# A fused expert-and-category kernel on one core: GpSimd's additions in runs tied to VectorE, a plan for them by slot, and the gate's sums in chosen slots

## The chip, the core and the metric

The kernel runs on one core of one Trainium2 chip. The metric is device time in microseconds of one execution; three executions of the kernel before took 2267.85, 2266.24 and 2268.05, median 2267.85. One more execution was profiled, and every duration below comes from it.

Names of engines: PE is TensorE (PEld its weight loads), DVE is VectorE, ACT is ScalarE, POOL is GpSimd, SP is SyncE, which issues nearly all DMAs. L871 is line 871 of the kernel before.

## What is computed

Two sequences of 2048 tokens with 512 features, all fp32. Cut to what matters:

```python
def dense(x, wi, wo):
    return relu(x @ wi) @ wo                    # 512 -> 2048 -> 512
s0 = dense(x, swi[0], swo[0])                   # two shared experts
s1 = dense(x, swi[1], swo[1])
eo = dense(x, wi[label[b]], wo[label[b]])       # one chosen expert for each sequence
gate_in = concatenate([eo[:, 0], s0[:, 0], s1[:, 0]])     # first token only
w = softmax(relu(gate_in @ g1) @ g2)            # 3 weights for each sequence
x = x + eo * w[0] + s0 * w[1] + s1 * w[2]
out = x + x @ W[cat[b]] + bias[cat[b]]          # a 512 x 512 layer for each sequence
```

## The kernel before

**Units.** Tokens are cut into 4 blocks of 1024. A unit is one expert on one block, 12 in all: units 0 to 3 are shared expert 0 on the four blocks, 4 to 7 shared expert 1, 8 and 9 the chosen expert of sequence 0, 10 and 11 that of sequence 1. Each unit has an up phase (`up`, 512 to 2048, relu) and a down phase (`down`, 2048 to 512).

**Fast multiplication.** Each product is done by two nested levels of a scheme with 7 block products in place of 8, paid for with sums and differences of blocks. So there are sums of the weights (`Prep`), sums of x (`x_sums`), sums of the hidden values (`make_tops` L701 to L708, `outer_sum` L871, the wide sums L744), and sums of results (L783 to L813 in the up phase, L914 to L933 in the down phase, `y_sums` L877). An up phase is 7 outer items in the order 1, 6, 2, 5, 7, 4, 3, each of 14 slots (`SEQ_UP`): 98 slots of 4 matmul instructions (L766), some 0.86 us each. A down phase is 49 slots (`SLOTS_DN`) of 8 matmul instructions (L900), some 1.73 us each, named by item and inner product: (7, y5) is slot 24, (4, x6) slot 43, (4, y5) slot 44. In an up phase items 1 and 5 "store" (ACT copies results out of PSUM), the others add results to an earlier block on DVE.

**The order of work is written by hand** (`tc.manual_schedule`). After each slot's matmuls and its evictions the program issues, in this order: wide sums, x sums (one step of `xg`), tops, the paced preparation (`prep_paced`), then one step of the background list `other_bg`. Each engine works its own list off in this order, and waits only for data and free buffers.

**Preparation of weights.** For shared expert 1 and both chosen experts (3 x 2 matrices of 4 groups each) `Prep` reads a group of raw weights by eight DMAs (L179, tile `pr`), makes 12 sums of it on GpSimd (L141: four `po`, four `ps`, four `pt`), and stores them to DRAM (L228) three slots after the last sum of each kind. 24 groups make 288 additions. `prep_paced` counts slots up by a rate (`RATE_UP` by item, `RATE_DN` by item) and issues one addition each time a whole one is reached; nothing but data and buffers holds the addition back on GpSimd. The first group of all is issued in unit 1, the last additions in unit 8. Of the 288, 59 are issued in down phases of units 1 to 7, and 29, 30, 29, 29, 29, 29, 29, 25 in the up phases of units 1 to 8.

**x sums.** Units 0 to 4 (`MAKES`) make the sums of their x block on GpSimd as they go (L370, L356), one item ahead of the matmuls that read them (`xi`, `xt`), and units 1 to 4 store them (`keep_parts`) for later units, which load them (`fetch_parts`).

**Weights of the matmuls** come by SP from DRAM into a pool of 12 tiles (`fetch_w`, L469 to L488); a load is issued when the tile twelve weights earlier has been used.

**Gate and layer 1.** When the chosen expert has done the first block of a sequence (units 8 and 10), `gate` and `layer1` of the block before are put in `other_bg`, one step of it a slot. The gate multiplies the rows of g1 by `gate_in` on DVE (twelve instructions, L1018 and L1020, one a slot from its ninth step on), sums over partitions by a matmul, multiplies by g2 (L1032, three), reduces all three at once (L1035), and makes the softmax (L1037 to L1047, with one Exp on ACT). `layer1` follows: 8 tiles, each with three scalings on ACT (L1112), three additions on GpSimd (L1117, `mix`), 4 matmuls (L1080, `po`) and one DVE addition with the bias (L1088). In unit 11, `premix` prepares the last block: it loads `acc` and four halves (`pm`), and adds them with 16 DVE instructions (L1158), one a step; what is left of `other_bg` at slot 47 of the last down phase is issued there. `last_mix` (L1170) adds the chosen expert's part tile by tile, and `last_layer1` ends the kernel with 64 `po` matmul instructions.

In unit 9 and unit 11 the gate's steps run from up item 1 slot 0 to item 3 of the order (item 2), slot 2; `layer1` from there to slot 4 of the down phase; in unit 11 `premix` from there to slot 32. In unit 10 there is `layer1` alone, up to the up phase's sixth item.

Of the kernel before, what the change touches and what calls it, by code (L numbers as in the profile page):

```python
# [8 lines left out]
F32 = mybir.dt.float32  # L9
AF = mybir.ActivationFunctionType  # L10
ALU = mybir.AluOpType
AX = mybir.AxisListType
# [3 lines left out]
P = 128  # L16
# [20 lines left out]
def cond_resid_kernel(  # L37
# [106 lines left out]
    class Prep:  # L144
# [89 lines left out]
        def step(self):  # L234

            self.flush(clock[0])
            done = bool(self.p) and (len(self.p) != 12 or clock[0] >= self.since + 6)
            if done:
                self.p.pop(0)()
            self.more()  # L240
            return done

        def more(self):
# [401 lines left out]

    pace = [0.0]

    def prep_paced(rate):
        clock[0] += 1
        if prep_bg:  # L650
            prep_bg[0].flush(clock[0])
        pace[0] = min(pace[0] + rate, 4.0) if prep_bg else 0.0
        while prep_bg and pace[0] >= 1 and prep_step():
            pace[0] -= 1

# [55 lines left out]
    def up(n, xg, tops, y):  # L711
# [12 lines left out]
        for j, i in enumerate(I_UP(n)):  # L724
# [32 lines left out]
            for s, (bk, k, d) in enumerate(SEQ_UP):  # L757
# [77 lines left out]
                if s in top_at:  # L835
                    next(tg, None)
                prep_paced(RATE_UP[j])
                step(other_bg)
# [10 lines left out]
    def down(n, H, tops, y, prepare):  # L849
# [124 lines left out]
        for s, (i, name) in enumerate(SLOTS_DN):  # L974
            if s in at:
                for _ in job:
                    pass
                job = jobs[at[s]]()
                y_sums(0, *sums.get(at[s], ()))
            elif s in second:  # L980
                y_sums(1, *sums.get(second[s], ()))
            slot(i, name)
            next(job, None)
            if name == "z2" and i != 1:
                next(job, None)
            prepare(s)
            prep_paced(RATE_DN[i])
            step(other_bg)
# [9 lines left out]
        nc.sync.dma_start(out=ys[slot_y, blk], in_=yf)  # L998

    gin = [const.tile([P, NX, DC], F32, name=f"gin_{b}") for b in range(B)]  # L1000
    gates = {}

    def gate(b, lag):
# [10 lines left out]
        for k in range(NX * DC):  # L1014
            j, c = divmod(k, DC)
            col = gin[b][:, j, c : c + 1]
            if k == 0:
                nc.vector.tensor_scalar(hid, g1t[j][:, c, :], col, None, ALU.mult)  # L1018
            else:
                nc.vector.scalar_tensor_tensor(hid, g1t[j][:, c, :], col, hid, ALU.mult, ADD)  # L1020
            yield
        for _ in range(3):
# [6 lines left out]
        yield  # L1029
        prod = bigp.tile([P, NX, D], F32, tag="o", bufs=1, name=f"prod_{b}")  # L1030
        for j in range(NX):
            nc.vector.tensor_tensor(prod[:, j, :], act, g2b[:, :, j], ALU.mult)  # L1032
            yield
        logit = small.tile([P, NX], F32, tag="logit", name=f"logit_{b}")
        nc.vector.tensor_reduce(logit, prod, AX.X, ALU.add)  # L1035
        mx = small.tile([P, 1], F32, tag="mx", name=f"mx_{b}")
# [98 lines left out]
    def premix(blk, lag):  # L1135
# [19 lines left out]
        for k, (j, h) in enumerate(parts):  # L1155
            for c in range(DC):
                o = acc["t"][c // 2][:, c % 2, h * 512 : (h + 1) * 512]
                nc.vector.scalar_tensor_tensor(  # L1158
                    o, got[k][:, c, :], gates[b][:, j : j + 1], o, ALU.mult, ADD
                )  # L1160
                yield
            if k == 0:
                fetch(3)
# [21 lines left out]

    RATE_UP = [0.36, 0.34, 0.34, 0.34, 0.18, 0.18, 0.34]
    RATE_DN = {1: 0.0, 2: 0.0, 3: 0.1, 7: 0.4, 6: 0.0, 5: 0.25, 4: 0.45}

    with tc.manual_schedule():
# [16 lines left out]
        for n, (e, blk) in enumerate(units):  # L1206
# [48 lines left out]
            if e >= 2:  # L1255
# [5 lines left out]
                if blk % NBB == 0:  # L1261
                    other_bg.append((f"g{b}", gate(b, 8)))
                if n + 1 < len(units):
# [34 lines left out]
```

## Time and profile before

| what | value |
|---|---|
| median of three runs | 2267.85 us |
| the profiled execution | 2268.57 us |
| its span, first to last instruction | 2266.8 us |
| mean granted TensorE clock | 0.995 |
| POOL L141 additions | 288, some 416 us in all |
| POOL x sums L370 | 140, 127 us |
| DVE adds with both operands in SBUF: L871, L744, L701 to L708 (t) | 192 x 1330, 96 x 1497, 288 x 1364 ns |
| DVE adds with one operand in PSUM: L789, L794, L813 | 240 x 686, 168 x 691, 168 x 687 ns |

A phase below is named by its stretch of the span in us. The page gives busy time and number of instructions of each engine; an answer by stretches gives the same for each stretch, with the granted clock, the DMA share and GB/s at the end of the line. An answer for one line of the kernel gives its instructions with their least, median and greatest duration in ns, and the first and last start. A list of waits says which engine stood still for which instruction, how long in total, how often, and the longest time. PE's busy time has modelled ends: single matmuls of 128x256 are shown with some 380 ns and start 216 ns apart, so the length of a phase says more than PE's busy time in it.

### The profile page before, as it was taken

What the parts mean: (1) busy time and instruction counts of PE and PEld (TensorE: products, weight loads), DVE (VectorE), ACT (ScalarE), POOL (GpSimd) and SP (SyncE); (2) the same over time, 40 slices, a digit from 0 to 9 for tenths busy, and PEclk for the clock granted to TensorE, in tenths of its full rate; (3) what the DMA queues carried; (4) which work ended last, traced back from release to release, by engine and by line L of the source; (5) the groups of instructions that cost most, each with busy time, mean ns of one, the idle gap of its engine ahead of it and who ended that gap; (6) DMA issues with size and microseconds to landing.
All of it is one profiled execution on the core that took longest, in us unless ns stands there. A gap on an engine that the chain in (4) does not pass through costs nothing.

```text
span 2266.8 us, 28546 instructions
## 1 busy us (share of the span) xinstructions
PE 2200.3 (97%) x9808; PEld 1852.5 (82%) x9808; DVE 1662.8 (73%) x2010; ACT 545.3 (24%) x937; POOL 790.5 (35%) x598
## 2 busy tenths in 40 slices
PE   8899999999999999999999999999999999999999
PEld 6787888888888888788888888888877877887686
DVE  7897787678588688588588588577676746857685
ACT  3221231331321320131231131131133133213310
POOL 6777543642752752332153233230032023002300
PEclk9999999999999999999999999999999999999999
DMA  9543997997996997796996896895896697579671
GB/s 339 194 172 98 354 316 231 305 324 233 339 327 191 309 309 218 262 321 191 292 324 184 281 330 189 291 326 161 285 310 187 185 306 239 154 239 326 211 274 56
DMA packets 483339, 577.22 MB, mean 255 GB/s; under 512 B 28280, under 2 KB 316024, under 8 KB 479740
## 3 DMA queue, kind: packets, MB, share of 16 engines
q1 hardware_dynamic: 478924, 567.53, 77.6%
q10 hardware_dynamic: 4272, 7.87, 1.0%
q8 instruction: 80, 1.31, 0.2%
q14 instruction: 63, 0.52, 0.1%
HBM read 417.47 MB, written 157.81 MB: 254 GB/s over the span
## 4 chain that ended last, share of the span: by engine, by line
PE 75%; DVE 11%; DMA 4%; issue 2%; POOL 1%; SPq 1%; ACT 0%; POOLq 0%; DVEq 0%; ACTq 0%
PE dx L900 21%; PE ux L766 19%; PE dy L900 11%; PE uy L766 9%; PE dz L900 5%; PE po L1080 5%; PE uz L766 5%; DVE h L871 2%; DVE y L877 1%; DVE t L701 1%; DVE t L706 1%; DVE t L704 1%; DMA w<-ws_s 1%; DMA g1raw<-in_L_cond_g_dram 1%; DVE hid L1020 1%
## 5 line engine op out<-in xcount | busy, mean ns | idle before, releaser
L900 PE MATMUL dx<-t,w 128*128 128x256 f32 x1680 | 399.4, 381 | 10.6 <-DVE ds L922 10.3
L766 PE MATMUL ux<-xs,w 128*128 128x256 f32 x1568 | 376.5, 381 | 10.4 <-DVE sm L1043 3.2
L900 PEld LDWEIGHTS dx<-t,w 128*128 128x128 f32 x1680 | 318.3, 190 | 58.8 <-DVE ds L922 12.4
L766 PEld LDWEIGHTS ux<-xs,w 128*128 128x128 f32 x1568 | 295.2, 190 | 66.3 <-DVE us L789 7.8
L1117 POOL TENSOR_TENSOR mix<-mix 128x512 f32<-128x512 f32 x72 | 101.4, 1409 | 536.9 <-ACT mix L1112 354.7
L141 POOL TENSOR_TENSOR po<-pr 128x384 f32<-128x384 f32 x48 | 59.3, 1250 | 601.1 <-DMA w<-ws_t 211.6
L871 DVE TENSOR_TENSOR h<-h,h 128x1024 f32<-128x1024 f32 x192 | 252.5, 1330 | 0.0
L789 DVE TENSOR_TENSOR us<-ux,h 128x512 f32<-128x512 f32 x240 | 162.3, 686 | 119.2 <-PE ux L766 118.9
L738 ACT ACTIVATE h<-h 128x1024 f32<-128x1024 f32 x156 | 164.5, 1056 | 239.3 <-DVE h L794 112.8
L766 PE MATMUL ux<-xi,w 128*128 128x256 f32 x808 | 192.2, 381 | 15.2 <-DVE us L789 6.2
L794 DVE TENSOR_TENSOR h<-uy,us 128x512 f32<-128x512 f32 x168 | 116.0, 691 | 120.8 <-ACT us L787 116.6
L766 PE MATMUL uy<-xs,w 128*128 128x256 f32 x784 | 187.7, 380 | 4.2 <-DVE h L813 2.4
L800 ACT ACTIVATE h<-uz 128x512 f32<-128x512 f32 x168 | 99.6, 593 | 380.7 <-PE uz L766 372.6
L766 PEld LDWEIGHTS ux<-xi,w 128*128 128x128 f32 x808 | 151.9, 190 | 41.7 <-issue 13.3
L900 PE MATMUL dy<-h,w 128*128 128x256 f32 x672 | 162.3, 385 | 11.9 <-DVE y L924 11.9
L766 PEld LDWEIGHTS uy<-xs,w 128*128 128x128 f32 x784 | 148.4, 190 | 30.6 <-DVE h L813 4.6
L900 PEld LDWEIGHTS dy<-h,w 128*128 128x128 f32 x672 | 128.3, 192 | 32.4 <-DVE y L924 9.8
L813 DVE TENSOR_TENSOR h<-uy,us 128x512 f32<-128x512 f32 x168 | 113.0, 687 | 52.0 <-PE uy L766 49.8
L744 DVE TENSOR_TENSOR h<-h,h 128x1024 f32<-128x1024 f32 x96 | 143.7, 1497 | 6.5 <-ACT h L800 5.1
L900 PE MATMUL dx<-h,w 128*128 128x256 f32 x616 | 146.3, 380 | 0.0
L900 PE MATMUL dz<-h,w 128*128 128x256 f32 x616 | 145.6, 379 | 0.1
L900 PE MATMUL dy<-t,w 128*128 128x256 f32 x576 | 136.1, 379 | 0.0
(153 smaller groups left out, 3365.5 us busy)
## 6 DMA issues: line engine op xcount, KB each, us to landing
w<-ws_t SPq DMA_DIRECT2D x352, 256.0 KB, 4.1
w<-ws_s SPq DMA_DIRECT2D x270, 256.0 KB, 4.2
w<-ws_o SPq DMA_DIRECT2D x264, 256.0 KB, 5.2
xs<-xs SPq DMA_DIRECT2D x49, 896.0 KB, 7.2
ws_s<-ps SPq DMA_DIRECT2D x24, 1024.0 KB, 7.7
ws_t<-pt SPq DMA_DIRECT2D x24, 1024.0 KB, 7.8
ys<-y SPq DMA_DIRECT2D x11, 2048.0 KB, 8.5
ws_o<-po SPq DMA_DIRECT2D x24, 768.0 KB, 7.4
```

The source lines that it names most:

```text
L141: eng.tensor_tensor(o, i0, i1, op)
L738: nc.scalar.activation(v, v, AF.Relu)
L744: nc.vector.tensor_tensor(o, blk_of(O[22], cc), blk_of(O[21], cc), ADD)
L766: nc.tensor.matmul(p[:, g, :], lhsT=wt[:, 2 * d + g, :], rhs=x_ops[n, i, k], start=first and g == 0, stop=True, skip_group_check=True,)
L789: nc.vector.tensor_tensor(t, p, half(src, 12 if k == 6 else 22, d), ADD)
L794: nc.vector.tensor_tensor(half(dst, 22, d), bank["y", d], t, ADD)
L800: nc.scalar.activation(half(dst, 11, d), p, AF.Relu if i in final else AF.Copy)
L813: nc.vector.tensor_tensor(half(dst, 12, d), p, sn["b", d], ADD)
L871: nc.vector.tensor_tensor(bl(o), bl(i0), bl(i1), SUB)
L900: nc.tensor.matmul(p, lhsT=wt[:, g, :], rhs=op[g], start=first and g == 0, stop=True, skip_group_check=True,)
L1080: nc.tensor.matmul(po[t], lhsT=mixed[c], rhs=l1[blk][0][:, c, :], start=(c == 0), stop=(c == DC - 1),)
L1117: nc.gpsimd.tensor_tensor(m[:, 3, :, :], m[:, 3, :, :], m[:, j, :, :], ADD)
```

## The change

Three things change.

1. **Additions in runs, each tied to DVE.** `prep_paced` is split. `prep_tick` counts the slot and issues stores that are due. `prep_run(count)` issues up to `count` additions (and one more where some are owed, five owed at most). Ahead of the first one it has DVE write a one-element memset to `pulse`, and GpSimd read it by a one-element addition into `seen`, so that the run's additions come, on GpSimd, behind the DVE work issued before the memset. Also the begin of a next group of raw weights comes with a run, no longer with any slot. In the built program there are 139 such pairs.
2. **A plan by slot.** `RUN_UP` and `RUN_DN` replace the rates: in an up phase runs of 2 or 3 after slots 4 and 8 of each item, in a down phase 2 after (7, y5), and 2 each after (4, x6) and (4, y5) where the next unit makes no x sums. Units that make x sums (0 to 4) have a plan of their own: none in the first item, then 3 and 2, 2 and 1, 2 and 1, 3 and 2, 3 and 2, 3 and 3. In the built program 31 additions stand in down phases (2, 2, 3, 6, 6, 6, 6 in units 1 to 7), and 27, 27, 26, 27, 38, 38, 38, 36 in the up phases of units 1 to 8.
3. **Gate and premix.** The gate's products, multiplications by g2 and reductions are issued only when `quiet` is set: in slots 1, 2, 11, 12, 13 of an up item, and in any slot of a down phase; two products a step. The reduction is split in three. The lag is 6 for 8. `premix` issues two sums a step. In the built program the gate's steps now end at slot 0 of the fifth item (7) of unit 9's and unit 11's up phase, `layer1` ends at slot 30 of the down phase, and `premix` runs from slot 30 to slot 47, with its sums from slot 42 on and six of the 16 at slot 47.

The order of instructions on PE and ACT is otherwise as before.

```diff
+        def can(self):
+            return bool(self.p) and (len(self.p) != 12 or clock[0] >= self.since + 6)
...
-    pace = [0.0]
-
-    def prep_paced(rate):
+    PULSES = 64
+    pulse = const.tile([1, PULSES], F32, name="pulse")
+    seen = const.tile([1, 1], F32, name="seen")
+    pulses, debt = [0], [0]
+
+    def prep_tick():
         clock[0] += 1
         if prep_bg:
             prep_bg[0].flush(clock[0])
-        pace[0] = min(pace[0] + rate, 4.0) if prep_bg else 0.0
-        while prep_bg and pace[0] >= 1 and prep_step():
-            pace[0] -= 1
+
+    def prep_run(count):
+
+        if not prep_bg:
+            return
+        debt[0] = min(debt[0] + count, 5)
+        most = count + 1
+        ready = False
+        while prep_bg and debt[0] and most:
+            if prep_bg[0].can() and not ready:
+                k = pulses[0] % PULSES
+                pulses[0] += 1
+                mark = pulse[:, k : k + 1]
+                nc.vector.memset(mark, 0.0)
+                nc.gpsimd.tensor_tensor(seen, mark, mark, ADD)
+                ready = True
+            if not prep_step():
+                break
+            debt[0] -= 1
+            most -= 1
...
-                prep_paced(RATE_UP[j])
+                prep_tick()
+                prep_run(RUN_UP[n in MAKES][j].get(s, 0))
+                quiet[0] = s in (1, 2, 11, 12, 13)
                 step(other_bg)
...
-            prep_paced(RATE_DN[i])
+            prep_tick()
+            prep_run(RUN_DN[n + 1 in MAKES].get((i, name), 0))
+            quiet[0] = True
             step(other_bg)
...
+            while not quiet[0]:
+                yield
             if k == 0:
                 nc.vector.tensor_scalar(hid, g1t[j][:, c, :], col, None, ALU.mult)
             else:
                 nc.vector.scalar_tensor_tensor(hid, g1t[j][:, c, :], col, hid, ALU.mult, ADD)
-            yield
+            if k % 2:
+                yield
...
         for j in range(NX):
+            while not quiet[0]:
+                yield
             nc.vector.tensor_tensor(prod[:, j, :], act, g2b[:, :, j], ALU.mult)
             yield
-        logit = small.tile([P, NX], F32, tag="logit", name=f"logit_{b}")
-        nc.vector.tensor_reduce(logit, prod, AX.X, ALU.add)
+            while not quiet[0]:
+                yield
+            nc.vector.tensor_reduce(logit[:, j : j + 1], prod[:, j : j + 1, :], AX.X, ALU.add)
+            yield
...
                     o, got[k][:, c, :], gates[b][:, j : j + 1], o, ALU.mult, ADD
                 )
-                yield
+                if c % 2:
+                    yield
...
-    RATE_UP = [0.36, 0.34, 0.34, 0.34, 0.18, 0.18, 0.34]
-    RATE_DN = {1: 0.0, 2: 0.0, 3: 0.1, 7: 0.4, 6: 0.0, 5: 0.25, 4: 0.45}
+
+    RUN_UP = {
+        False: [{4: 3, 8: 3}] * 3 + [{4: 3, 8: 2}] * 4,
+        True: [{}, {4: 3, 8: 2}, {4: 2, 8: 1}, {4: 2, 8: 1}] + [{4: 3, 8: 2}] * 2 + [{4: 3, 8: 3}],
+    }
+    RUN_DN = {
+        False: {(7, "y5"): 2, (4, "x6"): 2, (4, "y5"): 2},
+        True: {(7, "y5"): 2},
+    }
...
-                    other_bg.append((f"g{b}", gate(b, 8)))
+                    other_bg.append((f"g{b}", gate(b, 6)))
```

## The prediction

> **What bounds the kernel now.** I read the page first, then the costs of single operations, then the phases, then the waits of TensorE. A unit is one up phase (98 slots) and one down phase (49 slots); its bounds are the first `ux` and `dx` matmuls of the timeline.
>
> ```profile
> PE 2200.3 (97%) x9808; PEld 1852.5 (82%) x9808; DVE 1662.8 (73%) x2010; ACT 545.3 (24%) x937; POOL 790.5 (35%) x598
> ```
>
> TensorE is the bound, so only time in which it waits can be won. Phases (from:to, us, then busy us of PE, PEld, DVE, ACT, POOL):
>
> ```profile
> 832.20:926.00 93.80, 87.19 (x393) 75.78 (x393) 70.97 (x76) 9.95 (x25) 21.75 (x12) 0.96 0.68 207
> ...
> 1011.30:1097.10 85.80, 84.80 (x393) 74.35 (x392) 68.68 (x76) 9.99 (x25) 20.03 (x12) 1.00 0.69 209
> 1097.10:1183.90 86.80, 85.23 (x394) 74.28 (x394) 59.65 (x79) 29.44 (x42) 33.56 (x24) 1.00 1.01 326
> 1183.90:1271.40 87.50, 85.13 (x394) 74.30 (x393) 71.15 (x76) 10.00 (x25) 23.67 (x12) 1.00 0.67 204
> ...
> 1357.80:1446.70 88.90, 86.60 (x394) 75.57 (x393) 70.82 (x76) 10.04 (x25) 19.69 (x10) 0.98 0.68 210
> ...
> 1533.40:1618.00 84.60, 84.60 (x393) 74.47 (x392) 62.81 (x76) 10.02 (x25) 0.00 (x0) 1.00 0.59 175
> 1618.00:1736.30 118.30, 113.71 (x453) 84.71 (x452) 78.01 (x113) 44.81 (x68) 33.19 (x24) 1.00 0.88 294
> ...
> 1824.40:1939.60 115.20, 114.06 (x459) 86.56 (x458) 66.56 (x92) 44.82 (x66) 33.60 (x24) 1.00 0.85 271
> ```
>
> The down phase of unit 8 has no POOL work and takes 84.6 us; those of units 4 to 7 run the same 76 DVE instructions with 10 to 12 POOL additions and take 93.8, 85.8, 87.5 and 88.9. DVE is busy 8 us longer in them for the same work. Why, the instructions show (ns min/median/max):
>
> ```profile
> L871 DVE TENSOR_TENSOR h<-h,h x192: 1209/1218/2287, 127.9 to 2213.7; 128x1024 f32<-128x1024 f32 x192
> ...
> L789 DVE TENSOR_TENSOR us<-ux,h x240: 673/687/693, 40.8 to 2135.7; 128x512 f32<-128x512 f32 x120
> ...
> L141 POOL TENSOR_TENSOR ps<-pr x48: 1256/1277/2313, 217.9 to 1492.2; 128x512 f32<-128x512 f32 x48
> ```
>
> DVE's add of two SBUF tiles goes from 1.22 to 2.29 us, its add with a PSUM operand (`us<-ux`) never moves. The timeline of unit 4 shows both engines stretched together, and that POOL runs its 12 additions as one burst as soon as the raw weights land:
>
> ```profile
> 899.17 2.28 DVE L701 TENSOR_TENSOR t<-h 128x1024 f32<-128x1024 f32 x1
> 901.48 2.17 DVE L704 TENSOR_TENSOR t<-h,t 128x1024 f32<-128x1024 f32 x1
> ...
> 902.54 2.25 POOL L141 TENSOR_TENSOR ps<-ps,pr 128x512 f32<-128x512 f32 x1
> 904.86 2.12 POOL L141 TENSOR_TENSOR ps<-pr,ps 128x512 f32<-128x512 f32 x1
> ```
>
> There follows the longest wait of TensorE (us in total, times, longest), that for `y`:
>
> ```profile
> PE dy L900 <- DVE y L924: 11.9, 7, 6.3
> PE dx L900 <- DVE ds L922: 11.0, 11, 2.3
> ...
> PE ux L766 <- POOL xi L370: 1.2, 2, 0.9
> ```
>
> At the end, DVE is full exactly while premix (L1158) runs, and free after it:
>
> ```profile
> 2180.00:2195.00 15.00, 15.00 (x71) 13.20 (x70) 15.00 (x19) 2.29 (x6) 0.00 (x0) 1.00 0.78 275
> 2195.00:2210.00 15.00, 12.53 (x55) 9.77 (x54) 14.93 (x22) 1.14 (x3) 0.00 (x0) 1.00 0.42 122
> ...
> 2223.00:2235.50 12.50, 12.50 (x60) 11.00 (x59) 5.95 (x13) 0.77 (x2) 0.00 (x0) 1.00 0.00 0
> ```
>
> **What the Trainium skill says.** "SBUF — State Buffer", Who interferes with whom: a DVE instruction with two SBUF inputs contends with a GpSimd instruction that reads SBUF, one with at most one SBUF input doesn't, and the later one is blocked. The trace agrees (1.22 to 2.29 us against an unmoved 0.69). "TensorE: Matmul & The Clock Gate", Architectural detail: VectorE and GpSimd are strict FIFOs, so everything behind a waiting pulse waits too. "VectorE: DVE Perf Modes", The TRN2 errata: an fp32 tensor_tensor takes (N+151)/0.96 ns; 512 gives 691 (trace 687), one element 158.
>
> **Part 1, the pulses.** 139 memsets on DVE and 139 one-element adds on POOL, counted in the built program. No row shows them. DVE: the trace's reciprocal of one column took 0.16, like the 158 above; 139 x 0.16 = 22 us; DVE idles 25 to 30% of these phases and hides most of it. I take 2 us on the path (bounds 0 and 10; no gain is in a memset as such). POOL: from 128x256 at 0.73 and 128x512 at 1.28, one element is about 0.19: 26 us of an engine 35% busy, 0 on the path unless POOL fills up (rival 3). The new wait: POOL's one-element add stands until DVE has worked off what was issued before the memset. Behind it queue the run's additions, then x sums (L370, L356) of units 1 to 4, for which TensorE waits 2.5 slots into the next item; and SP waits for what those write.
>
> **Part 2, where the 288 additions go.** By the program 59 of them stood in down phases of units 1 to 7 and 31 do now: 2, 2, 3 in units 1 to 3, 6 in each of 4 to 7. Four of the six follow (4, x6) and (4, y5), where DVE has only PSUM adds and y_sums (L877) left; two at (7, y5) still meet the tops.
> - Down, units 4 to 7: 9.2 + 1.2 + 2.9 + 4.3 = 17.6 over 84.6. About a fifth of the meetings remain: 3.5. Gain 14 (bounds 9 and 17). Late next is DVE's own chain, which unit 8 hides wholly.
> - Down, units 1 to 3: 90.0, 89.0, 86.3. The first two hold 32 transposes of about 0.11 (3.5 us), so 1.9, 0.9, 1.7 are lost. x sums remain there: gain 2.
> - Up, units 1 to 4 (86.5, 89.6, 87.0, 87.4): 12.1 lost over 84.6. Item 1 of such units gets no additions and x sums come first, but they meet the wide sums as before: gain 2 (bounds -8 and 8). Units 5 to 8 (85.3, 86.8, 86.4, 86.7): 6.8 lost; they now take 38, 38, 38, 36 additions for 29, 29, 29, 25. A burst after slot 4 is over by slot 9; one after slot 8 (2 or 3 x 1.28, begun about 2 us late behind DVE's queue) lasts to slot 13 and meets wide sums at 11. I take 0 (bounds -4 and 5).
> - SP: a store of prepared weights is issued 3 slots (2.6 us) after its last addition, which can now end 6 us after its slot. SP stands about 3 us, with weight loads, x stores and raw loads behind it. Weights are 12 tiles, 20 us, ahead and land in 4 to 5: hidden. Without that cover each stop costs its 3 us.
> - Raw loads (L179, eight for each of 24 groups) are issued from a run too, not from any slot. Each lands in 3.4 us (median), and the group's first addition comes 6 to 14 slots later (5 to 12 us): 0 on the path; a late group shifts a run toward the wide sums (rival 2). Both orders end in unit 8, so nothing is forced at its end.
>
> **Part 3, the gate.** Unit 9's up takes 118.3 with 453 matmuls, unit 10's 115.2 with 459; six po matmuls are 6 x 0.43 = 2.6, so a gate costs 118.3 - 112.6 = 5.7, twice 11.4. The twelve products (0.75 each) now go in pairs to slots 1, 2, 11, 12, 13; six in slots 11 to 13 are 6 x 0.66 = 4.0 us of DVE beside 1.2 of its `h` sums, four more in slots 1 and 2 are 2.7 beside 1.2 of `uz`: 9.1 us of work in the 7.7 of nine slots, so DVE is about 1.5 behind at slot 4, and `sm` still waits for ACT's Exp. I leave 1.2 each: gain 9 (bounds 4 and 11). The shorter lag (6 for 8) costs 0: the first product now waits for slot 11 anyway, when the loads it used to wait 2.1 us for have landed. The split reduction adds 4 small instructions, within that.
>
> **Part 4, what the later gate pushes.** It ends 26 slots later (item 5 slot 0 instead of item 3 slot 2), and layer 1 with it: it ran to down slot 4 and now to slot 30. So 12 of 24 POOL mixes (four groups of three, 1.27 each) and 4 to 5 puts (0.69) fall among the tops and outer sums of the down phases of units 9 and 11. Units 5 to 7 lost 1.2 to 4.3 with 12 in longer bursts: 1.5 each, 3 in all (bounds 0 and 8). Unit 10 has no gate.
>
> **Part 5, the end.** premix starts 26 down slots later and its 16 sums stand in slots 42 to 47, six of them and four last_mix sums together at 47. DVE's pitch there is 0.66 and 0.42. From slot 42's eviction at 2225.1: 10.6 of sums, 1.7 of last_mix, 4.7 of its own work give the first finished tile near 2241, where TensorE wants it at 2235.5: +5.5. What premix cost at 2195 to 2210 (15.0 - 12.5 = 2.5) goes. Net +3 (bounds -2 and 9). Its loads keep their distance of ten slots and land in 8.2.
>
> **Sum.** -14 - 2 - 2 - 0 - 9 + 2 + 3 + 3 = -19. The profiled execution took 2268.57 (span 2266.8 and 1.8 around it), 0.7 above the median 2267.85. 2267.85 - 19 = 2249.
>
> **Rivals.**
> 1. Everything fits: the up phases recover 12 more and the tail 5: 2232. For it: unit 5's up lost only 0.7 with 24 additions. Against: the wide sums at slot 11.
> 2. The change doesn't separate the engines: a memset holds POOL back only until DVE gets there, and in items that store (1 and 5) DVE runs ahead, so bursts meet tops and wides after all; 12 of the 19 are given back: near 2261.
> 3. Slower: in items 5 and 6 of units 1 to 4 POOL has 5 additions, 4 x sums, 2 pulses: 5 x 1.28 + 4 x 0.73 + 0.4 = 9.7 of 12.1 us. If all are contended (2.28 and 1.72) it is 18.7, 6.6 late in each of two items, less 2.2 of lead: 11 a unit. At three quarters of that, 32 in four units: 2281. It decides from a mean addition of about 1.75 us. Against: `xi` waits are 1.2 us now.
>
> **Chances.** Forecast 0.61 (2238 to 2259), rival 1 0.14, rival 2 0.14, rival 3 0.11. A measurement tells 0.2% (4.5 us) from no change. Faster: 0.61 + 0.14 + 0.08 of rival 2; same 0.06; slower 0.11. The range 2230 to 2264 leaves out rival 3 and the edges.
>
> **What would show it.** Right: down phases of units 4 to 7 near 85.5, L871's and L701's means near 1.25, unit 9's up near 114 after its po matmuls are counted, a DVE full to the end of unit 11 and a gap before the last po matmuls. Wrong: TensorE waits for `xi` or for `w` above 5 us, or up phases of units 5 to 8 beyond 88.

## The result, and the profile after

The changed kernel takes 2287.34 us (median of 6 runs, 2282.66 to 2288.25) against 2267.95 for the kernel before: ratio 1.0075, 95% interval 1.0064 to 1.0086. By the medians it is slower by 19 us (14.5 to 19.5 by the interval) where 19 us less were forecast. Lines shift: L766 before is L789 after, L871 is L896, L744 is L767, L900 is L925.

The engines' busy times, from the page after:

```profile
PE 2199.9 (96%) x9808; PEld 1854.9 (81%) x9808; DVE 1676.0 (73%) x2153; ACT 545.1 (24%) x937; POOL 802.3 (35%) x737
```

TensorE's busy time over the whole span is what it was (2200.3 before), and the span is 18.4 us longer. The phases (from:to, length, busy us of PE, PEld, DVE, ACT, POOL with their instructions, clock, DMA share, GB/s): down of units 4 and 5, up and down of 6, down of 7 and 8, then up and down of 9:

```profile
837.00:922.20 85.20, 85.12 (x393) 74.33 (x393) 66.31 (x79) 10.03 (x25) 11.23 (x11) 1.00 0.76 239
1009.10:1099.80 90.70, 87.00 (x393) 75.40 (x392) 70.38 (x80) 9.98 (x25) 20.41 (x18) 0.98 0.74 227
1099.80:1187.70 87.90, 85.47 (x393) 74.15 (x392) 59.62 (x100) 29.38 (x42) 41.09 (x45) 1.00 1.02 332
1187.70:1284.60 96.90, 89.27 (x394) 76.69 (x393) 73.20 (x79) 10.00 (x25) 24.28 (x24) 0.95 0.68 208
1371.10:1459.50 88.40, 86.50 (x393) 75.53 (x392) 68.88 (x79) 10.01 (x25) 18.71 (x16) 0.98 0.71 219
1547.30:1631.90 84.60, 84.60 (x393) 74.47 (x393) 62.85 (x76) 10.03 (x25) 0.00 (x0) 1.00 0.66 200
1631.90:1734.50 102.60, 98.36 (x421) 79.13 (x421) 72.11 (x110) 37.62 (x56) 15.59 (x12) 1.00 0.89 296
1734.50:1838.30 103.80, 102.07 (x433) 82.02 (x433) 75.11 (x82) 17.35 (x37) 23.43 (x12) 1.00 0.61 187
```

Unit 4's down phase came out as forecast (93.8 to 85.2). Those of units 5, 6 and 7 hold 18, 24 and 16 GpSimd instructions where the plan has six additions and their pulses, and take 90.7, 96.9 and 88.4. The waits of TensorE tell what is new in them (us in total, times, longest; L925 are the down phases):

```profile
PE dz L925 <- DMA w<-in_L_cond_swo_dram: 8.4, 2, 5.9
PE dx L925 <- DMA w<-ws_o: 1.9, 2, 1.6
PE ux L789 <- DMA w<-ws_s: 1.4, 1, 1.4
PE uy L789 <- DMA w<-ws_o: 0.9, 1, 0.9
```

Weights are late, 13 us with the small ones, all but 0.3 of it in units 5 to 8. The longest wait cost more than its own length. After it the granted clock is at half for a while, and three us hold 9 matmuls in place of 15:

```profile
1214.00:1217.00 3.00, 3.00 (x9) 2.37 (x8) 0.00 (x0) 0.00 (x0) 0.00 (x0) 0.50 0.99 327
1220.00:1223.00 3.00, 3.00 (x15) 2.64 (x14) 2.10 (x4) 0.35 (x1) 0.00 (x0) 1.00 0.74 252
```

So unit 6's down phase takes 12.3 us more than unit 8's 84.6: 7.5 of waits, and 4.7 by which PE is busy longer (89.27) at a mean clock of 0.95. Units 5 to 8 together take 709.7 for 692.0: TensorE's waits for weights grew from 2.0 to 12.7 there, those for VectorE stayed at some 8, and PE's busy time grew from 682.0 to 688.4. Why the weights are late, SyncE's timeline across unit 6 shows (start, us the issue takes):

```profile
1178.47 4.50 SPq L179 DMA_DIRECT2D pr<-in_L_cond_wi_dram  x8
...
1185.07 0.94 SPq L486 DMA_DIRECT2D w<-in_L_cond_swo_dram  x2
1192.71 0.53 SPq L228 DMA_DIRECT2D ws_o<-po  x1
1193.33 0.83 SPq L476 DMA_DIRECT2D w<-ws_o  x1
1200.85 0.52 SPq L228 DMA_DIRECT2D ws_s<-ps  x1
1201.46 1.89 SPq L486 DMA_DIRECT2D w<-in_L_cond_swo_dram  x1
1203.57 5.28 SPq L179 DMA_DIRECT2D pr<-in_L_cond_wi_dram  x8
```

Between 1186.0 and 1192.7, and between 1194.2 and 1200.9, SyncE stands at a store (L228) whose additions GpSimd has not done; the weight load behind it starts at 1201.5, and TensorE stands 5.9 us for it, until 1208.0. The Trainium skill says where such a wait is served under "DMA: Bandwidth & Descriptors", Anatomy of one DMA, a section written for transfers that GpSimd issues: "any semaphore wait happens on the issuing sequencer before dispatch". The trace agrees for SyncE: two stops of 6.7 us with loads behind them. GpSimd, in the same stretch (start, us):

```profile
1186.42 1.00 POOL L141 TENSOR_TENSOR po<-pr 128x384 f32<-128x384 f32 x1 [10.21 <-DMA w<-ws_o]
1187.38 1.17 POOL L672 TENSOR_TENSOR seen<-pulse 1x1 f32<-1x1 f32 x1
...
1198.69 2.13 POOL L141 TENSOR_TENSOR ps<-pr,ps 128x512 f32<-128x512 f32 x1
```

The group's raw loads were issued from 1178.5 and landed from 1183.0 on, and its first addition ran at 1186.4, after GpSimd had stood idle 10.2 us (the profile puts that wait down to a weight load, which the addition does not read). Several pulse adds take 1.17 instead of 0.18, each beside a sum of VectorE. All stops of SyncE at these stores for GpSimd (total, times, longest), before:

```profile
SPq L228 <- POOL ps L141: 11.9, 8, 8.6
SPq L228 <- POOL po L141: 11.4, 7, 3.3
SPq L228 <- POOL pt L141: 1.8, 3, 1.1
```

and after:

```profile
SPq L228 <- POOL ps L141: 26.6, 14, 6.6
SPq L228 <- POOL po L141: 26.2, 9, 7.1
SPq L228 <- POOL pt L141: 7.9, 5, 2.8
```

They grew from 25 to 61 us: from 10 to 24 in units 5 to 8, from 15 to 37 in units 1 to 4. The contention of VectorE with GpSimd did not fall as a whole: L896's mean is 1330 ns, as L871's was, and L767's is 1577 for 1497. What is new is L767's longest (min/median/max, ns):

```profile
L767 DVE TENSOR_TENSOR h<-h,h x96: 1199/1226/4592, 72.7 to 2121.1; 128x1024 f32<-128x1024 f32 x96
```

A sum of VectorE that waits out four GpSimd instructions in a row, in unit 3's up phase:

```profile
646.96 0.18 POOL L672 TENSOR_TENSOR seen<-pulse 1x1 f32<-1x1 f32 x1
647.10 1.27 POOL L141 TENSOR_TENSOR ps<-pr 128x512 f32<-128x512 f32 x1
647.46 4.59 DVE L767 TENSOR_TENSOR h<-h,h 128x1024 f32<-128x1024 f32 x1
648.34 1.26 POOL L141 TENSOR_TENSOR ps<-ps,pr 128x512 f32<-128x512 f32 x1
...
649.57 0.71 POOL L373 TENSOR_TENSOR xi<-x 128x256 f32<-128x256 f32 x1
650.25 0.71 POOL L373 TENSOR_TENSOR xi<-x,xi 128x256 f32<-128x256 f32 x1
```

And the end, as forecast: the last po matmuls wait for last_mix.

```profile
2252.22 8.12 PE L1117 MATMUL po<-w,acc 128*128 128x512 f32 x15 [4.09 <-DVE acc L1208]
```

### The profile page after: what moved, and what is told of

Same layout as the page of the kernel before. It is cut to its first block, busy times and chain, and to the rows that moved or that the text cites. A ratio compares the mean times of both kernels' runs of the same rounds, so it can differ in the third digit from the quotient of the medians.

```text
span 2285.2 us, 28896 instructions
## 1 busy us (share of the span) xinstructions
PE 2199.9 (96%) x9808; PEld 1854.9 (81%) x9808; DVE 1676.0 (73%) x2153; ACT 545.1 (24%) x937; POOL 802.3 (35%) x737
## 4 chain that ended last, share of the span: by engine, by line
PE 52%; DVE 6%; DMA 4%; issue 1%; SPq 1%; POOL 0%; ACT 0%; POOLq 0%; ACTq 0%; DVEq 0%
PE dx L925 15%; PE ux L789 12%; PE dy L925 8%; PE uy L789 5%; PE po L1117 5%; PE dz L925 4%; PE uz L789 3%; DVE h L767 1%; DMA g1raw<-in_L_cond_g_dram 1%; DVE h L836 1%; DMA w<-ws_o 1%; DMA w<-in_L_cond_W_dram 1%; DVE hid L1051 0%; DVE acc L1195 0%; DMA mix<-ys 0%
## 5 line engine op out<-in xcount | busy, mean ns | idle before, releaser
L925 PE MATMUL dx<-t,w 128*128 128x256 f32 x1680 | 400.4, 381 | 4.2 <-DVE ds L947 2.3
L789 PE MATMUL ux<-xs,w 128*128 128x256 f32 x1568 | 373.3, 380 | 13.6 <-DVE uz L806 8.6
L925 PEld LDWEIGHTS dx<-t,w 128*128 128x128 f32 x1680 | 320.1, 191 | 53.5 <-DVE ds L947 3.9
L789 PEld LDWEIGHTS ux<-xs,w 128*128 128x128 f32 x1568 | 296.4, 190 | 65.7 <-DVE uz L806 12.2
L1154 POOL TENSOR_TENSOR mix<-mix 128x512 f32<-128x512 f32 x72 | 111.6, 1552 | 540.5 <-DVE us L812 350.5
L672 POOL TENSOR_TENSOR seen<-pulse 1x1 f32<-1x1 f32 x139 | 58.0, 417 | 614.8 <-DVE pulse L671 583.6
L896 DVE TENSOR_TENSOR h<-h,h 128x1024 f32<-128x1024 f32 x192 | 252.8, 1330 | 0.0
L789 PE MATMUL ux<-xi,w 128*128 128x256 f32 x808 | 193.3, 382 | 15.2 <-DVE us L812 6.4
L789 PE MATMUL uy<-xs,w 128*128 128x256 f32 x784 | 186.5, 380 | 2.4 <-DVE h L836 1.4
L789 PEld LDWEIGHTS ux<-xi,w 128*128 128x128 f32 x808 | 153.2, 191 | 41.6 <-issue 16.0
L789 PEld LDWEIGHTS uy<-xs,w 128*128 128x128 f32 x784 | 148.3, 190 | 27.3 <-DVE h L836 3.6
L925 PE MATMUL dy<-h,w 128*128 128x256 f32 x672 | 160.6, 382 | 6.3 <-DVE y L949 5.8
L925 PE MATMUL dz<-h,w 128*128 128x256 f32 x616 | 149.9, 387 | 10.3 <-DMA w<-in_L_cond_swo_dram 8.4
L767 DVE TENSOR_TENSOR h<-h,h 128x1024 f32<-128x1024 f32 x96 | 151.4, 1577 | 3.9 <-ACT h L823 2.6
L925 PEld LDWEIGHTS dy<-h,w 128*128 128x128 f32 x672 | 127.2, 191 | 27.9 <-issue 9.4
L925 PE MATMUL dx<-h,w 128*128 128x256 f32 x616 | 145.5, 379 | 0.0
L925 PEld LDWEIGHTS dz<-h,w 128*128 128x128 f32 x616 | 119.0, 194 | 27.9 <-issue 9.2
```

The costliest lines, as they stand in the source:

```text
L672: nc.gpsimd.tensor_tensor(seen, mark, mark, ADD)
L767: nc.vector.tensor_tensor(o, blk_of(O[22], cc), blk_of(O[21], cc), ADD)
L789: nc.tensor.matmul(p[:, g, :], lhsT=wt[:, 2 * d + g, :], rhs=x_ops[n, i, k], start=first and g == 0, stop=True, skip_group_check=True,)
L896: nc.vector.tensor_tensor(bl(o), bl(i0), bl(i1), SUB)
L925: nc.tensor.matmul(p, lhsT=wt[:, g, :], rhs=op[g], start=first and g == 0, stop=True, skip_group_check=True,)
L1154: nc.gpsimd.tensor_tensor(m[:, 3, :, :], m[:, 3, :, :], m[:, j, :, :], ADD)
```

## Experiments

Stage lengths below run from the first `ux` matmul of one unit to that of another, in each run's profile (us). Units 1 to 4 and 5 to 8 are the stages with additions.

| kernel | time | ratio to before (95%) | units 1-4 | units 5-8 | unit 9 on |
|---|---|---|---|---|---|
| before | 2267.95 | | 709.6 | 692.0 | 648.8 |
| after | 2287.34 | 1.0064-1.0086 | 706.9 | 709.7 | 653.3 |
| e1 no pulses | 2277.71 | 1.0028-1.0058 | 695.7 | 708.2 | 653.4 |
| e2 gate only | 2271.27 | 1.0007-1.0028 | 709.6 | 688.6 | 653.0 |
| e3 raw from any slot | 2281.25 | 1.0044-1.0070 | 709.1 | 699.9 | 654.7 |
| e4 raw once | 2266.30 | 0.9984-1.0003 | 710.9 | 685.7 | 655.0 |
| e5 before, raw once | 2256.93 | 0.9945-0.9973 | 706.9 | 682.1 | 649.1 |
| e6 untied | 2300.20 | 1.0129-1.0173 | 711.6 | 716.7 | 653.2 |
| e7 stores late | 2279.44 | 1.0046-1.0073 | 697.2 | 695.4 | 662.9 |
| e8 mixed | 2269.02 | 1.0003-1.0021 | 695.6 | 701.8 | 648.9 |
| e9 no pulses, stores late | 2276.64 | 1.0022-1.0050 | 694.5 | 701.9 | 663.8 |
| e10 "best" | 2269.20 | 0.9997-1.0013 | 693.1 | 698.9 | 656.6 |
| e11 before, stores late | 2258.12 | 0.9943-0.9972 | 699.4 | 688.8 | 650.0 |
| e12 gate, lag 8 | 2274.58 | 1.0014-1.0031 | 711.2 | 691.6 | 656.0 |
| e13 before, stores late 2 | 2260.66 | 0.9953-0.9984 | 708.0 | 685.6 | 649.3 |
| e14 mixed, stores late 2 | 2264.53 | 0.9977-0.9993 | 697.6 | 698.2 | 649.4 |
| e15 GpSimd adds only | 2301.78 | 1.0121-1.0159 | 713.8 | 718.8 | 654.6 |
| e16 memsets only | 2273.45 | 1.0017-1.0048 | 696.4 | 705.0 | 653.4 |

Each ratio is to executions of the kernel before taken along with that run (medians 2266.53 to 2268.70), so it isn't always the quotient of the times shown. Before, e2 and e12 have the same program in units 1 to 8: their stages differ by up to 3.4, which is what a difference of two profiles can't tell. A stage length comes from one profiled execution, and some of these stand off their kernel's median: e7's is 5.2 us below it, e8's 3.9 and e2's 2.3 below, e4's and e12's 4.1 and e15's 2.6 above; the others lie within 2.

My theory after the trace (A): raw weights land after their run is due, so that additions, stores and weight loads slide. Its rival (B): the pulses cost by their wait. Theories E and G below are about the stores, C, D and F are rivals to one run each. Where an edit is longer, `...` stands for the rest of it.

**e1**, no pulses:

```
-                nc.vector.memset(mark, 0.0)
-                nc.gpsimd.tensor_tensor(seen, mark, mark, ADD)
...
```

> The changed kernel without the memsets and one-element adds, plan and gate as changed. Theory A (raw weights land after their run is due, so most groups start when they land and the pulses hold nothing back that matters): same as the changed kernel, 2283 to 2291. Theory B (the waits for the pulses are what makes it slow, GpSimd stands 584 us in them): 2265 to 2272. If pulses do help as forecast, slower than 2292.

2277.71: between the two. Units 1 to 4 give 11 us back, units 5 to 8 nothing (their waits for `swo` weights even rise to 13.6). Two causes in two stages. Stops at stores fell from 37 to 5 us in units 1 to 4 and not in units 5 to 8.

**e2**, the kernel before with the new gate and premix alone (parts 3 to 5).

> The kernel before with the new gate and premix alone. The forecast's own terms (-9 for the gate, +3 for mixes moved down, +3 at the end): 2265. Theory A from the two traces (units 9 and 10 unchanged, unit 11 4.2 longer): 2272. The difference to the changed kernel is then what the additions cost, 15 to 22.

2271.27, as A: this part costs 3.7 (2 to 6 by the interval), where the sum had -3.

**e3**, raw loads from any slot:

```
         if prep_bg:
             prep_bg[0].flush(clock[0])
+            if prep_bg[0].over():
+                prep_bg.pop(0)
+        if prep_bg:
+            prep_bg[0].more()
```

> The changed kernel, but a next group of raw weights is begun from any slot, as soon as its buffer is free, not only with a run. Theory A, in the form that the begin is late: groups meet their runs, the waits for w in the down phases of units 5 to 7 (about 10 us) go, 2265 to 2275. Theory A in the form that the DMA engines are full in the up phases (share 1.02 to 1.04 in units 6 to 8): the loads land hardly earlier, 2280 to 2290. Theory B: 2283 to 2291.

2281.25: units 5 to 8 win 10. An earlier issue helps, but only in part.

**e4**, one raw group in four loaded:

```
...
-            for c in range(DC):
+            for c in range(DC) if g == 0 else ():
```

It leaves out 240 of the 320 raw loads, so it is a bound and no complete kernel. A group is eight loads of 128 KB, 1 MB, and not the 2 MB of the expectation.

> The changed kernel, with only the first of the four groups of each matrix loaded; the additions of the other three work on the same raw tile (so the prepared weights are other numbers, and 18 of 24 groups move 2 MB less each). Theory A: GpSimd never waits for raw weights, additions stay in their slots, stores are not late: 2245 to 2258. Theory B: the pulses and the fuller up phases cost the same as before, 2278 to 2288.

2266.30. Units 5 to 8 fall by 24, their down phases to 84.6 to 85.8; units 1 to 4 stay. SyncE stands at stores longer than ever here (73 us, 28 of them in units 5 to 8), and TensorE doesn't wait for weights in units 5 to 8 at all. So a stop alone costs little; that it costs where the loads behind it have no lead left is argued, not shown. The edit takes away the lateness of raw weights and their share of the DMA at once; no run separates these two.

**e5**, the same edit in the kernel before, again a bound.

> The kernel before, with only the first of each four groups of raw weights loaded (the other three groups add the same tile again, so the prepared weights, and the output, are other numbers; the additions, stores and slots are unchanged). It is the control for the same edit in the kernel after, which took 24 us off units 5 to 8 there. Theory A (the 17 us that units 5 to 8 lost come from raw weights that land after the additions of the new plan are due, which the old pacing avoided): the old pacing has little to win from it, 2258 to 2266, units 5 to 8 at 686 to 691. Rival C (the loads themselves cost the same in both orders, by the share of the DMA engines they take): units 5 to 8 fall by as much as in the kernel after, to about 670 to 675, and the total to about 2247.

2256.93. Units 5 to 8 fall by 9.9, neither A's few us nor C's as much as after. Both orders pay for the raw loads, the new one 14 more. Without them the two orders differ there by 3.6 only.

**e6**, untied:

```
-                nc.gpsimd.tensor_tensor(seen, mark, mark, ADD)
+                nc.gpsimd.tensor_tensor(seen, ones[0:1, 0:1], ones[0:1, 0:1], ADD)
```

> The kernel after, with GpSimd's one-element add reading a constant in place of the tile that VectorE has just set: memsets and one-element adds all stay, only the wait between the engines goes. Theory B (what the pulses cost, 11 us in units 1 to 4, is GpSimd standing for VectorE's queue): as with no pulses at all, 2275 to 2280, units 1 to 4 at 695 to 699. Rival D (it is the instructions themselves, 139 on each engine, and the slots of the queue they take): as the kernel after, 2284 to 2289, units 1 to 4 at 704 to 708.

2300.20: worse than both. Theory B falls: with the adds in place the wait wins 13 us, and something in the pulses costs more than it wins.

**e7**, stores 12 slots after the last addition:

```
-                        self.late.append((clock[0] + 3, part, g, own[part]))
+                        self.late.append((clock[0] + 12, part, g, own[part]))
```

> The kernel after, with the stores of prepared weights issued 12 slots after the group's last addition in place of 3: SyncE no longer stands at a store whose additions aren't done, with weight loads behind it. Theory E (the waits of TensorE for weights in the down phases of units 5 to 7 come from SyncE standing at these stores): those waits (8.4 us) go, and of the 17 us lost in units 5 to 8 about 8 come back: 2276 to 2280, units 5 to 8 at 699 to 703. Rival F (the sixteen DMA engines are full there, so weights come late whoever waits where): no change, 2284 to 2289, with the waits for weights still above 6 us. Worse than 2290 if the next group's additions then wait for the tiles that late stores still hold.

2279.44. As E and more: the `swo` waits are gone, the stops fall from 61 to 3.4 us (two of 6.1 and 8.1 us at raw loads are new), units 5 to 8 win 14.3 and units 1 to 4 win 9.7. The profiled execution is a fast one: by the medians the whole kernel wins 7.9, by the profiles 12.8, so the 14.3 may be 9. It loses 10 in unit 9, where the last stores now stand ahead of the gate's loads, SyncE again:

```profile
1611.27 5.04 SPq L228 DMA_DIRECT2D ws_s<-ps  x1
1616.40 4.18 SPq L228 DMA_DIRECT2D ws_t<-pt  x1
1620.63 3.60 SPq L1037 DMA_DIRECT2D g1raw<-in_L_cond_g_dram  x1
```

**e8**, the new plan without pulses up to unit 4, old pacing with raised rates from unit 5, old gate:

```
...
+    RATE_UP = [0.41, 0.40, 0.40, 0.40, 0.30, 0.30, 0.40]
```

> A version put together from what the runs showed: units 1 to 4 take the new plan without the pulses, units 5 to 8 the old pacing with rates raised so that the 30 additions which the plan takes out of units 1 to 4 fit in (36 to 37 for each up phase, 8 for each down phase), with gate and premix as before. If the two parts are independent: units 1 to 4 at 695 to 698 (as with no pulses), units 5 to 8 at 692 to 697, 2254 to 2260 in all. If it is the number of additions in units 5 to 8 and not the form of the plan that makes the weights late: units 5 to 8 at 704 to 710, about 2268 to 2272.

2269.02. Units 1 to 4 as expected; units 5 to 8 at 701.8, between the two: nearer to a price for the number of additions. SyncE's stops there are 24 us, as many as after.

**e9**, e1 and e7 together.

> The kernel after without its pulses and with the stores of prepared weights issued 12 slots after a group's last addition in place of 3: the two edits that each brought something back, together. Theory G (both act in one place: the pulses hold additions back, the additions end after the slot of their store, and SyncE stands at the store with the loads behind it): late stores alone already brought units 1 to 4 to 697, so taking the pulses away too changes little there, 694 to 698, and units 5 to 8 stay at 692 to 697; about 2274 to 2280, of which some 10 us are the last group's stores in front of the gate's loads in unit 9. Rival B (pulses cost by themselves): units 1 to 8 gain a further 8 to 11, 2265 to 2271.

2276.64: with late stores, taking the pulses away gives 2.8 where it gave 9.6. As G in units 1 to 4 (694.5) and in all; units 5 to 8, at 701.9, are 5 above its range. They are also 6.5 above e7's; but e7's profiled execution is 5.2 us below its median and e9's 1.2 above, so this may be no more than the choice of execution.

**e10**, plan without pulses, late stores (those of the last part after 3), old gate.

> The new plan of slots without pulses, stores 12 slots late but those of the very last part after 3 as before, gate and premix as in the kernel before. If the parts found so far are independent: units 1 to 4 at 696, units 5 to 8 at 693 to 697, units 9 on at 649, 2252 to 2259 in all, faster than both kernels. If late stores lose their gain without the pulses (additions early, tiles held longer by late stores): 2264 or more.

2269.20, a miss of the first branch, by number in the second: the last additions end in unit 8's down phase, since a part with late stores lets the next begin 9 slots later, and unit 9 still loses 8.

**e11**, the kernel before with late stores (same exception).

> The kernel before with stores 12 slots late (the last part's after 3). Theory G says that standing at stores is what the new plan adds, because it issues several additions in one slot; with the old pacing of about one addition in three slots the stores find their tiles done. So little is to be had: 2262 to 2268. If the old order also lost time at stores: 2255 or less.

2258.12, the fastest complete kernel here, between the two branches and below G's: the old order seems to have lost time at its stores too. But the edit also moves additions (unit 4's down phase: 4 GpSimd instructions for 12, and 84.6 us for 93.8).

**e12**, e2 with `layer1(blk, 8 if blk % NBB == 0 else 14)`.

> The kernel before with the new gate and premix (2271 in an earlier run), and layer 1 of the blocks with a gate given a lag of 8 slots in place of 14, so that premix begins 6 slots earlier in unit 11. If the loss of the gate part sits in the late premix (TensorE waits 4.1 us for the last mixed tile): that wait goes and the run takes 2266 to 2268. If it sits in the mixes among the down phases' sums and in TensorE's wait for layer 1's weights: 2270 to 2273, or worse where the weights have less time to land.

2274.58, a miss, though its interval meets e2's. The 4.1 us wait at the end is gone, and a wait of 4.3 for `y` in unit 11's down phase and 3.0 for `mix` in its up phase are there instead: in both places tried, TensorE waits for VectorE or GpSimd.

**e13** and **e14**, the kernel before and e8 with stores late but for each part's last group, so that no addition moves:

```
-                        self.late.append((clock[0] + 3, part, g, own[part]))
+                        self.late.append((clock[0] + (12 if self.todo else 3), part, g, own[part]))
```

> The kernel before with the stores of prepared weights 12 slots late, except each part's last group, which keeps 3, so that the next part begins when it did and the last stores don't stand in front of the gate's loads in unit 9. Theory G (SyncE's stand at stores is a cost in the old order too): as the run with all stores late, 2258, less the 2 to 3 us that it lost in unit 9: 2254 to 2259; unit 4's down phase near 85 again. If that gain was a chance of the shifted additions: 2264 to 2268, unit 4's down phase near 93.

> The mixed version (new plan without pulses in units 1 to 4, old pacing with raised rates from unit 5 on, gate and premix as before; 2269 in an earlier run) with the stores late in the same way. If plan and stores add up: units 1 to 4 at 693 to 696, units 5 to 8 at 688 to 693 (they had 702), 2248 to 2257 in all. If the 30 additions which the plan moves into units 5 to 8 cost by themselves: units 5 to 8 at 697 or more, 2260 to 2266.

e13: 2260.66, between its two ranges; stops at stores fall from 25 to 5 us (one of 8.8 us at raw loads is new), units 5 to 8 win 6.4, unit 4's down phase stays at 93.3. So the stops are a cost of their own in the old order; unit 4's loss isn't theirs. e14: 2264.53; units 5 to 8 at 698.2, 12.6 above e13, as the second answer has it. But it is no clean price. Fifteen us of stops are left in these units:

```profile
SPq L228 <- POOL po L141: 14.5, 4, 4.6
```

And TensorE loses by another way than after. It waits 0.6 us for weights there and 14.1 for VectorE, where e13 has none and 4.8: the down phases of units 5 to 7 hold 15, 24 and 20 additions (e13: 12, 11 and 8) among VectorE's sums. So the moved additions cost through VectorE here, and through late weights after; e8 has both (9.2 and 6.7).

**e15**, only GpSimd's adds (reading `ones`); **e16**, only the memsets.

> The kernel after with only GpSimd's one-element adds left, reading a constant: no memset, no tie. If it is GpSimd's adds that cost (each is one more instruction that takes turns with VectorE's sums): near the untied kernel, 2294 to 2302. If it is the memsets on VectorE: near the kernel with no pulses, 2275 to 2281.

> The kernel after with only VectorE's memsets left: nothing on GpSimd, no tie. If it is GpSimd's adds that cost: near the kernel with no pulses, 2275 to 2282 (139 memsets of 59 ns are 8 us of VectorE, which idles a quarter of these phases). If it is the memsets: 2294 to 2302.

2301.78 and 2273.45: it is the adds. They cost 24 us over e1; the memsets nothing that e16's interval can tell from e1's. The wide sums of e1, e15 and e16 (min/median/max):

```profile
L760 DVE TENSOR_TENSOR h<-h,h x96: 1207/1226/2342, 74.8 to 2111.2; 128x1024 f32<-128x1024 f32 x96
```

```profile
L764 DVE TENSOR_TENSOR h<-h,h x96: 1207/1230/5545, 72.8 to 2137.1; 128x1024 f32<-128x1024 f32 x96
```

```profile
L765 DVE TENSOR_TENSOR h<-h,h x96: 1199/1226/2340, 72.6 to 2107.3; 128x1024 f32<-128x1024 f32 x96
```

In e1 and e16 no wide sum is more than 1.2 us over its median; in e15, with the adds, one is 4.3 us over it.

## Why the prediction was wrong

**Parts 3 to 5, gate, mixes, end: -9, +3, +3 forecast; -4, +4, +4 measured.** What the up phases of units 9 and 11 take beyond their matmuls (84.6 us and 0.43 for each po) fell from 8.0 and 7.9 to 6.0 and 6.0. By the prediction's own measure, the excess over unit 10's up phase, a gate's 5.7 fell to 3.4 (102.6 less 99.2, which is unit 10's 115.5 without 38 po of 0.43): "I leave 1.2 each" was the wrong term. TensorE's wait for `sm` (1.6) is gone there, and it now waits 1.7 for `uz` and 1.4 for `us`. The down phases lost 2.0 each, the end 4.2: mechanisms right, sizes near (the end's sum, as the prediction writes it, comes to 2242.1 and not 2241). The sum, +4, is e2's +3.7.

**Part 1, the pulses: +2 forecast, 10 measured** (after less e1, 9.6). The prices were not the fault: a memset took 59 ns (I had 0.16 us; the 158 ns of one element was an estimate, from a formula for a tensor_tensor and not for a memset), a free GpSimd add 183 (0.19). Nor was the strict order of the queues: GpSimd's adds did stand for their pulses, 583.6 us in 66 waits, and taking that wait away alone made it worse (e6). The step that failed is "26 us of an engine 35% busy, 0 on the path unless POOL fills up": it costed a GpSimd instruction by its own length. With the adds, sums of VectorE stand for several GpSimd instructions in a row: 24 us (e15 over e1). That it is the add's reading of SBUF is argued; no run put an instruction there that reads none. Holding GpSimd back, what the tie is for, wins 13 (e6 less after). Net 10, most of it through late additions and stops, it seems: stops at stores in units 1 to 4 are 37 us with the tie, 10 with the adds untied (e6) and 5 without pulses (e1), and with late stores 2.8 are left (e9 against e7).

**Part 2, the slots.** Where the plan only moved additions off VectorE's sums it did what was forecast. In e1 down phases 1 to 3 won 2.8 (forecast 2), up phases 1 to 4 2.5 (2), both within what two profiles can't tell, and unit 4's down phase 8.5, which is clear of it. One reading in this part was wrong without a price that shows: "DVE has only PSUM adds and y_sums (L877) left" after (4, x6) and (4, y5), but a y sum (L902 now) reads SBUF twice, and where those runs stand in units 4 to 7 one took 2.5 to 4.4 us for its median of 0.69; in unit 7 TensorE didn't wait for it. In e1 units 5 to 7 lost 15 in their down phases (after: 14) instead of winning their share of the 14, about 7. Three steps of the prediction failed there:

- "they now take 38, 38, 38, 36 additions for 29, 29, 29, 25 [...] I take 0". That line holds the move that mattered: with the six in each down phase, 30 of the 288 additions leave units 1 to 4 for units 5 to 8. I costed VectorE's meetings only. Two and a half groups go with them, each with eight raw loads of 128 KB and stores of 1024, 1024 and 768 KB: about 9.8 MB, by an estimate 30 us of the whole DMA at the 330 GB/s of these up phases, which were full before (share 1.00 to 1.01 in units 6 to 8; 1.02 to 1.04 now). Price: 9.8 (e7 against e13, with few stops at stores; the tie and its adds are in it, and e7's execution is a fast one), 16.3 (e9 against e13, without tie and adds), 3.6 where raw weights need not be loaded (e4 against e5). In the old pacing, with stops in it, 9.8 (e8 against before) and 12.6 (e14 against e13).
- "Raw loads [...] 0 on the path". They are issued from a run, by a SyncE of which one issue can take 3 us there (a weight load at 1173.2 took 3.20), and the next run finds them not landed: GpSimd idles 10.2 us ahead of a group, and the group falls into the down phase. e3, which issues them earlier, and e4, which leaves most of them out, win 10 and 24 in units 5 to 8.
- "SP stands about 3 us [...] hidden". I named what it costs without the cover, 3 us a stop, and stopped there. The stops are up to 7.1 us, two follow each other, and raw loads sit in the same queue, so the next group is late as well. Their price in units 5 to 8 is 14.3 after, or 9 (e7), and 6.4 before (e13).

So units 5 to 8, +17.7: by e7 and e13 9.8 for what was moved into them and 7.9 more for stops. This split is not settled: by the runs without pulses it is 16 and nothing (e1 is 16.2 above before, e9 16.3 above e13). What the traces show is the way it is paid: 10.7 more of waits for weights and 6.5 more of PE's busy time, as at the half clock above; the prediction put the first at nothing and had no term for the second. Units 1 to 4, -2.7: -14 for the plan, +11 for the pulses. With unit 0 (-1.1) and the +4.5 from unit 9 on, this is the 18.4 of the span.

**The rivals.** The third had the sign, not the cause: TensorE's waits for `xi` stayed at 1.4 us. The second holds in part, since bursts did meet the tops in units 5 to 7, though by late raw weights. Of the signs I gave against me, the wait for `w` above 5 us came true; up phases of units 5 to 8 stayed below 88 (86.5 to 87.9). "Both orders end in unit 8, so nothing is forced" held, and did not help.

**What stays open.** How the 13 us of the tie divide over its slots; whether e9 and e10 really stand 6.5 and 3.5 above e7 in units 5 to 8, and with it how the 17.7 divide; whether a version exists that keeps the 14 of units 1 to 4 without moving additions into units 5 to 8. The gain to be had at once is in e11: late stores in the old order, 0.3 to 0.6% faster than the kernel before.

## What to carry to other kernels

When work is rescheduled, count it per stage before and after, with its loads and stores: what leaves one stage arrives in another, and there the DMA may be full, as here. A wait inserted on one engine can be paid on the queue that waits for that engine; here SyncE stood at stores with weight loads behind them, and issuing a store later, when its data is sure to be there, took 7 to 11 us off the kernel before (e13, e11), where the plan added 19. Price an instruction added to a helper engine by what it does to the engine beside it, not by its length alone: 139 adds of 0.18 us cost 24. And price a stage length only after looking where its profiled execution stands among the others.

## What the runs showed of the hardware

- One-element GpSimd adds lengthened VectorE's sums. In units 1 to 8 no sum of two SBUF tiles took over 2.4 us in e1, e9, e11 and e16; after, e15 and e6 had 16, 20 and 23 of them, up to 5.9 us. At the same time GpSimd's additions got shorter (mean 1.49 us in e1, 1.33 in e15): the adds change who waits, not only how long. The kernel before has one such sum (5.3 us, beside five GpSimd instructions, three x sums among them), and e2 one of 5.6, so it isn't the pulses alone that can do it; why GpSimd then goes several times in a row, no run here shows. The Trainium skill's "SBUF — State Buffer", Who interferes with whom, has the first to issue keep the shared port for its whole instruction and the other block; in the timeline of unit 3 above the sum that began at 647.46 is also passed by three GpSimd additions that began after it, at 648.34, 649.57 and 650.25, and there the measurement decides.
- After some waits of TensorE the granted clock was at half: in unit 6's down phase (waits of 5.9 and 1.6 us) the mean is 0.95 and PE is busy 4.7 us longer than in unit 8's; in unit 4's before (6.3 us) 0.96 and 2.6 us. What length of wait brings it, these runs don't tell: unit 7's down phase after has one of 1.9 us at 0.98.
- A one-element memset on VectorE took 59 ns and cost nothing measurable, 139 times (e16).
- The one-element GpSimd add took 183 ns alone and 1.17 to 1.22 us beside a sum of VectorE.
